# State-space mixer: the identity additions of two pairs of state columns issued together, behind every second pair

## Chip, cores and metric

The kernel runs on one core of one Trainium2 chip. The metric is the device time of one execution in microseconds; the comparison is between the kernel before and the kernel with the change below.

The engines are called by the names of the profile: PE is TensorE's matrix unit (PEld its weight loads), DVE is VectorE, ACT is ScalarE, POOL is GpSimd, SP is the engine that issues most transfers.

## What is computed

The whole program is a Perceiver-like stack of eleven layers over a (2, 256, 256) input and a (2, 4096, 256) context, all in float32. The change touches one layer, the state-space mixer. Cut to what matters, the reference of that layer is:

```python
delta = softplus(dtr @ W_dt + 2.0 * dt_bias).reshape(b, l, G, D_STATE)   # G = 32, D_STATE = 16
A = -exp(A_log).reshape(G, D_STATE, D_STATE)
a = exp(delta[..., None] * A)                       # decay of each state
bb = (delta * x)[..., None] * Bg[:, :, :, None, :]  # drive of each state
_, h = associative_scan(comb, (a, bb), axis=1)      # h[t] = a[t] * h[t-1] + bb[t]
y = einsum('blgpn,blgn->blgp', h, Cg)               # sum over the 16 state columns n
y = (y + D * xf) * silu(z)
return y @ W_out
```

There are 512 inner channels (four blocks of 128), 16 state columns per channel and 2 x 256 tokens. For each block and each state column the kernel makes a decay, a drive, a scan along the tokens, a product with C, and a sum over the 16 columns.

## The kernel before

The layer lies in one function, `l1_attn`. Channels lie on the 128 partitions, the 512 tokens (two sequences of 256) along the free dimension. The loop runs over 32 "pairs": a pair `k` is a block `j` of channels and two of its 16 state columns, so eight pairs make a block (k = 0 to 7 is block 0, and so on).

For a pair, five helper functions issue the work:

- `b_columns(k)` (L1332, L1340): two 32-row matmuls on PE spread the B values of the two columns over the partitions into two banks of the tag "tr" (two banks in all), and ACT copies each into a "spread" tile.
- `drives(k)` (L1349, L1351): ACT writes the decay exp(delta * A) of each column into a bank of the tag "dec" (two banks in all), POOL multiplies the spread tile by delta * x. Behind that it issues one step of the softplus of later blocks (`later`: an addition on ACT, L1224, and a product on POOL, L1225) as long as there are such steps.
- `states(k)` (L1332, L1365, L1369, L1370): two 32-row matmuls on PE spread the C values into two banks of the tag "mm" (three banks in all); DVE runs four scans (two columns, two sequences) into "state" tiles, and multiplies each column's state by its C bank. The order on DVE is scan, scan, scan, product of the first column (L1369), scan, product of the second column (L1370).
- `add_up(k)` (L1377): two matmuls with the identity on PE add the two weighed states into the bank `sums[j]` of the tag "acc" (one bank). Behind the eighth pair of a block DVE adds D * x (L1381) and POOL multiplies by silu(z) (L1384).
- `made` gives, in the first five iterations, one step each of the projections for blocks 1 to 3 (matmuls through L358, ACT copies L1292, L1295, L1296).

A float32 matmul stands as two passes in the trace, so a pair has four passes for its C columns, four for B columns and four for its additions.

Weighed states lie in tiles of the tag "state" in a pool of six buffers, so three pairs' worth; a tile comes free when the identity matmul that reads it has run. The loop is skewed: iteration `k` issues states of pair k, B columns of pair k + 2, decays and drives of pair k + 1, a step of `made`, and the additions of an earlier pair. The block stands under `in_order`, which ties each instruction of PE, DVE, ACT and POOL to the one issued before it on the same engine, so the order in the code is the order on each engine. The lines of the loop around the change:

```python
for k in range(-2, n + 1):          # n = 32
    if 0 <= k < n:
        states(k)
    if k + 2 < n:
        b_columns(k + 2)
    if 0 <= k + 1 < n:
        drives(k + 1)
    step = next(made, None)
    ...
```

After the loop `conv_hidden` issues the first matmuls of the next layer, and `linear` multiplies by W_out.

Of the kernel before, what the change touches and what calls it, by code (L numbers as in the profile page):

```python
# [268 lines left out]
class Perceiver:  # L269
# [960 lines left out]
    def l1_attn(self, x):  # L1230
# [5 lines left out]
        with ExitStack() as s:  # L1236
# [98 lines left out]
            def b_columns(k):  # L1335
                got = columns(mats["b"], bT, *pairs[k], "tr")
                spread[k] = []
                for ps in got:
                    spread[k].append(p4.tile([P, T], F32, name="spread", tag="spread"))
                    nc.scalar.copy(spread[k][-1], ps)  # L1340

            def drives(k):
                j, q, rs = pairs[k]
                decay[k], drive[k] = [], []
                for r, b in zip(rs, spread.pop(k)):

                    a = self.bank([P, T], "dec")
                    n = 16 * j + 4 * r + q
                    nc.scalar.activation(a, delta[:, j, :], AF.Exp, scale=neg_a[:, n : n + 1])  # L1349
                    decay[k].append(a)  # L1350
                    nc.gpsimd.tensor_mul(b, dx[:, j, :], b)  # L1351
                    drive[k].append(b)
                step = next(later, None)
                if step is not None:
                    step()

            def states(k):
                got = columns(mats["c"], cT, *pairs[k], "mm")
                weighed[k] = []

                for i, (a, bb) in enumerate(zip(decay.pop(k), drive.pop(k))):
                    h = p4.tile([P, T], F32, name="state", tag="state")
                    weighed[k].append(h)
                    for b in range(B):
                        nc.vector.tensor_tensor_scan(  # L1365
                            h[:, ts(b, L)], a[:, ts(b, L)], bb[:, ts(b, L)], 0.0, ALU.mult, ALU.add
                        )
                        if (i, b) == (1, 0):
                            nc.vector.tensor_mul(weighed[k][0], got[0], weighed[k][0])  # L1369
                nc.vector.tensor_mul(h, got[1], h)  # L1370

            def add_up(k):
                j, q, rs = pairs[k]
                if k % 8 == 0:
                    sums[j] = self.acc([P, T])
                for i, h in enumerate(weighed.pop(k)):
                    nc.tensor.matmul(  # L1377
                        sums[j], self.ident, h, start=k % 8 == 0 and i == 0, stop=k % 8 == 7 and i == 1
                    )
                if k % 8 == 7:  # L1380
                    nc.vector.scalar_tensor_tensor(  # L1381
                        yz[:, j, :], xr[:, j, :], self.col("ssm_d", j), sums[j], ALU.mult, ALU.add
                    )
                    nc.gpsimd.tensor_mul(yz[:, j, :], yz[:, j, :], zs[:, j, :])  # L1384

            e = mybir.EngineType
            with self.in_order(e.PE, e.DVE, e.Activation, e.Pool):
                n = len(pairs)
                for k in range(-2, n + 1):
# [6 lines that stand above are left out]
                    step = next(made, None)  # L1396
                    if step is not None:
                        step()
                    if k > 0:
                        add_up(k - 1)  # L1400
                self.conv_hidden("tr", "tr", "dec")
                return self.linear(yz, wout, x)
# [1196 lines left out]
```

## Time and profile before

| what | value |
|---|---|
| three runs, median | 2589.68 us |
| three runs, lowest and highest | 2589.52 and 2592.2 us |
| profiled execution, own time | 2594.41 us |
| profiled execution, span of its instructions | 2592.6 us |
| mean granted TensorE clock in it | 0.957 |
| busy over the span: PE, DVE, ACT, POOL | 95%, 66%, 52%, 36% |
| first scan and start of the last L1381 of the layer | 1320.4 and 1451.9 us |

Shares of the whole span average over eleven layers with different limits; the loop of the mixer lies between 1320 and 1452 us and is some 5% of the time. So it is read from views that are cut to that stretch. A start in the timeline is counted from the span's start. "issue" as the end of an idle time means that the profile shows nothing that was waited for. Matmuls are pipelined: one pass of 512 columns is listed as about 0.59 us while the next one starts sooner, so on PE starts are compared with starts.

### The profile page before, as it was taken

To read this page: it belongs to the slowest core of one execution; us is meant where nothing else is said; L and a number is where in the kernel's file an instruction comes from. 1 tells how busy PE (TensorE), PEld (TensorE's weight loads), DVE (VectorE), ACT (ScalarE), POOL (GpSimd) and SP (SyncE) were. 2 spreads that over 40 slices of the span, in tenths; PEclk is the share of its full clock that TensorE was granted. 3 is DMA by queue.
4 is the path that set the end of the run, shared out by engine and by line. 5 is a ranking of instruction groups with operands and counts; after the bars stand their busy time and mean duration, and the time that the engine had idled before them with its cause. 6 is when DMAs were issued, how large, how long until landed. Compare 5 with 4: busy or idle time off the path is not lost.

```text
span 2592.6 us, 51423 instructions
## 1 busy us (share of the span) xinstructions
PE 2457.8 (95%) x20579; PEld 1637.4 (63%) x20581; DVE 1709.5 (66%) x3184; ACT 1342.6 (52%) x2540; POOL 921.2 (36%) x864
## 2 busy tenths in 40 slices
PE   8987999999999999999799988899999999999889
PEld 6854566666666666666533556457935666664678
DVE  5566577777777777777579655444367888844542
ACT  3323666666666666666466322332116777783512
POOL 0520256656656656656459322001101222210010
PEclk9988999999999999999899998789999999998789
DMA  6210422222242222222300100006630000004556
GB/s 259 90 58 24 125 67 66 74 66 66 74 123 74 74 66 67 74 69 82 122 9 1 65 21 25 1 25 256 238 138 18 2 2 2 2 2 148 196 221 219
DMA packets 77278, 214.62 MB, mean 83 GB/s; under 512 B 6408, under 2 KB 21456, under 8 KB 66544
## 3 DMA queue, kind: packets, MB, share of 16 engines
q1 hardware_dynamic: 72128, 202.69, 23.4%
q0 software_dynamic: 1888, 5.90, 0.7%
q8 instruction: 162, 2.65, 0.4%
q10 hardware_dynamic: 3024, 2.75, 0.3%
q14 instruction: 76, 0.62, 0.1%
HBM read 190.48 MB, written 20.84 MB: 82 GB/s over the span
## 4 chain that ended last, share of the span: by engine, by line
PE 41%; DVE 5%; issue 2%; ACT 2%; POOL 1%; DMA 0%; DVEq 0%; ACTq 0%; POOLq 0%; SPq 0%
PE ps_mm L358 10%; PE ps_mm L2181 5%; PE ps_tr L2225 5%; PE ps_tr L2209 4%; PE ps_tr L358 3%; PE acc L358 3%; PE ps_mm L785 2%; PE ps_tr L2344 1%; DVE state L1365 1%; PE acc L826 1%; PE ps_tr L2387 1%; POOL spread L1351 1%; PE ps_tr L801 1%; PE acc L1377 1%; PE acc L1592 1%
## 5 line engine op out<-in xcount | busy, mean ns | idle before, releaser
L1092 POOL TENSOR_TENSOR total<-total,S 128x512 f32<-128x512 f32 x434 | 543.0, 1284 | 273.8 <-ACT S L1081 273.3
L1081 ACT ACTIVATE S<-S 128x512 f32<-128x512 f32 x512 | 302.6, 625 | 209.4 <-DVE S L1078 209.0
L2185 DVE TENSOR_REDUCE mx<-ps_mm 128x1 f32<-128x512 f32 x512 | 317.7, 683 | 71.5 <-PE ps_tr L2209 54.3
L1067 DVE TENSOR_TENSOR most<-ps_mm,most 128x512 f32<-128x512 f32 x448 | 278.1, 683 | 115.7 <-ACT S L1064 115.7
L1078 DVE TENSOR_TENSOR S<-S,ps_dec 128x512 f32<-128x512 f32 x512 | 317.2, 677 | 1.7 <-PE ps_dec L1136 1.7
L1064 ACT COPY S<-ps_mm 128x512 f32<-128x512 f32 x512 | 262.6, 599 | 99.8 <-PE ps_mm L1057 99.7
L2213 ACT ACTIVATE PT<-ps_tr 128x512 f32<-128x512 f32 x476 | 246.8, 602 | 74.6 <-PE ps_tr L2209 71.9
L1017 PEld LDWEIGHTS ps_tr<-w_l1x_wv,ctxT 128*64 128x64 f32 x4096 | 235.4, 137 | 58.4 <-issue 57.7
L1057 PE MATMUL ps_mm<-qT,kT 64*128 64x256 f32 x2048 | 255.7, 389 | 0.0
L1104 PE MATMUL acc<-S,v 128*64 128x256 f32 x2048 | 252.2, 385 | 0.7 <-DVE rec L1142 0.7
L2181 PE MATMUL ps_mm<-kT,qT 32*128 32x512 f32 x1024 | 249.7, 617 | 0.2 <-DVE mx L2185 0.2
L1017 PE MATMUL ps_tr<-w_l1x_wv,ctxT 128*64 128x128 f32 x4096 | 248.2, 273 | 0.0
L1017 PE MATMUL ps_tr<-ctxT,w_l1x_wk 128*64 128x512 f32 x1024 | 242.4, 593 | 0.4 <-PE ps_mm L1017 0.4
L2209 PE MATMUL ps_tr<-qm,kT 32*128 32x256 f32 x1904 | 238.2, 388 | 0.0
L1057 PEld LDWEIGHTS ps_mm<-qT,kT 64*128 64x128 f32 x2048 | 187.3, 186 | 44.1 <-issue 18.6
L1104 PEld LDWEIGHTS acc<-S,v 128*64 128x64 f32 x2048 | 139.1, 136 | 95.6 <-ACT S L1064 38.8
L2209 PEld LDWEIGHTS ps_tr<-qm,kT 32*128 32x128 f32 x1904 | 170.9, 184 | 16.2 <-issue 6.2
L2234 POOL TENSOR_TENSOR sums<-sums,part 128x256 f32<-128x256 f32 x102 | 73.8, 724 | 256.9 <-ACT part L2233 256.9
L2225 PE MATMUL ps_tr<-PT,v 128*32 128x256 f32 x2048 | 139.6, 385 | 0.3 <-ACT PT L2213 0.3
L1017 PEld LDWEIGHTS ps_tr<-ctxT,w_l1x_wk 128*64 128x64 f32 x1024 | 75.8, 137 | 91.3 <-issue 74.7
L335 DVE COPY v<-ps_tr 128x512 f32<-128x512 f32 x120 | 82.8, 690 | 71.4 <-PE ps_tr L1017 71.3
L2181 PEld LDWEIGHTS ps_mm<-kT,qT 32*128 32x128 f32 x1024 | 86.1, 184 | 60.0 <-issue 48.4
(543 smaller groups left out, 3817.9 us busy)
## 6 DMA issues: line engine op xcount, KB each, us to landing
ctxT<-in_ctxT SPq DMA_DIRECT2D x144, 512.0 KB, 3.6
ctxT<-in_ctxT SPq DMA_DIRECT2D x16, 1024.0 KB, 6.8
w_l2f_gu<-in_l2f_gu SPq DMA_DIRECT2D x16, 1024.0 KB, 7.4
bd_dram<-bd SPq DMA_DIRECT2D x8, 1536.0 KB
w_l3f_w<-in_l3f_w SPq DMA_DIRECT2D x11, 1028.0 KB, 8.4
w_l3f_w<-in_l3f_w SPq DMA_DIRECT2D x11, 1024.0 KB, 5.1
ctx<-in_ctx SPq DMA_DIRECT2D x8, 1024.0 KB, 6.1
w_l2f_down<-in_l2f_down SPq DMA_DIRECT2D x16, 512.0 KB, 4.3
```

What stands on the lines that cost most here:

```text
L358: self.nc.tensor.matmul(out, lhsT, rhs, start=i == 0, stop=i == len(pairs) - 1)
L1017: nc.tensor.matmul(ps[part], a[:, part], b, start=k == 0, stop=k == len(pairs) - 1)
L1057: nc.tensor.matmul(banks[hh, i][:, j, :], k[part, ts(2 * i + j, P)], q[u][part, :], start=True, stop=True)
L1067: nc.vector.tensor_tensor(m, ps, m, ALU.max)
L1078: nc.vector.tensor_tensor(t, t, spread[u][:, hh, :].unsqueeze(1).to_broadcast([P, 2, L]), ALU.add)
L1081: nc.scalar.activation(t, t, AF.Exp)
L1092: nc.gpsimd.tensor_add(tot, tot, t)
L1104: nc.tensor.matmul(av[u][part], vs[:, 2 * i + j, part], got[hh, i][:, j, :], start=g % 8 == 0 and i + j == 0, stop=g % 8 == 7 and i + j == 2,)
L2181: nc.tensor.matmul(ps, qT[rows, 2 * half + c, ts(t, P)], kT[rows, ts(j, 512)], start=True, stop=True,)
L2185: nc.vector.tensor_reduce(mx[:, c, r, j : j + 1], ps, AX.X, ALU.max)
L2209: nc.tensor.matmul(ps[:, i, :], kT[rows, ts(2 * u + i, P)], q[rows], start=True, stop=True)
L2225: nc.tensor.matmul(ps[ts(r, 32), :], v[:, 2 * u + i, :], pt[:, i, :], start=i == 0, stop=i == 1)
```

## The change

The additions of a pair were issued in the iteration after the pair. Now those of two pairs are issued together, in every second iteration: in iteration k = 2, 4, ..., 32 the additions of pairs k - 2 and k - 1. The additions of odd pairs keep their place; those of even pairs come one iteration later, directly ahead of those of the odd pair. Everything else, the order of the additions into `sums[j]` included, stays.

```diff
@@ -1396,7 +1396,9 @@
                     step = next(made, None)
                     if step is not None:
                         step()
-                    if k > 0:
+
+                    if k > 0 and k % 2 == 0:
+                        add_up(k - 2)
                         add_up(k - 1)
                 self.conv_hidden("tr", "tr", "dec")
                 return self.linear(yz, wout, x)
```

## Prediction

> **What bounds the kernel now.** I read four views, in this order. First the busy time by stretches, restricted to the state stage (start us:end us, length, then busy us and count of each engine, the granted clock, DMA share):
>
> ```profile
> 1342.00:1362.00 20.00, 20.00 (x64) 6.96 (x64) 18.76 (x32) 14.96 (x27) 17.80 (x15) 1.00 0.01 2
> 1362.00:1394.00 32.00, 32.00 (x104) 11.39 (x104) 30.91 (x51) 22.47 (x39) 31.90 (x27) 1.00 0.00 0
> 1394.00:1425.00 31.00, 31.00 (x100) 10.98 (x96) 29.97 (x50) 21.07 (x36) 29.77 (x25) 1.00 0.00 1
> ```
>
> PE never idles in the middle of the stage, DVE is 94 to 97% busy, POOL is full from 1362 to 1394. Three engines are level, so the order matters. Second, one iteration of the timeline (start, duration):
>
> ```profile
> 1346.47 1.85 DVE L1365 TENSOR_TENSOR_SCAN state<-ps_dec,spread 128x256 f32<-128x256 f32 x3
> 1346.52 1.13 PE L1332 MATMUL ps_mm<-cT,mat_c 32*128 32x512 f32 x4
> ...
> 1347.48 1.02 PE L1332 MATMUL ps_tr<-bT,mat_b 32*128 32x512 f32 x4
> ...
> 1348.24 0.66 DVE L1369 TENSOR_TENSOR state<-ps_mm,state 128x512 f32<-128x512 f32 x1
> 1348.43 1.98 PE L1377 MATMUL acc<-state,ident 128*128 128x512 f32 x4
> 1348.54 1.07 ACT L1340 COPY spread<-ps_tr 128x512 f32<-128x512 f32 x2 [1.01 <-PE ps_tr L1332]
> ...
> 1349.49 1.32 ACT L1349 ACTIVATE ps_dec<-delta,neg_a 128x512 f32<-128x512 f32 x2
> ```
>
> Write S(k) for the first scan of pair k, C(k), B(k) and A(k) for its c columns, b columns and additions. C(5) starts at 1346.52, B(7) 0.96 later, A(4) 0.95 after that, C(6) at 1350.35: PE's iteration is 0.96 + 0.96 + 1.91 = 3.83 us. The chain that releases the next pair is C(5) at 1346.52, B(7), its copies at 1348.54, the exponential at 1349.49, S(6) at 1350.30: C to next S is 3.78.
>
> Third, DVE later on: S is at 1362.61, 1393.63, 1424.48 and 1446.86 for k = 9, 17, 25, 31. From k = 26 to 31 that is 3.73 per pair, DVE's own floor (scans and products start about 0.59 apart, the last product waits 0.78 for the last scan). A pair with L1381 behind it takes 4.38. So S(31) is set by PE at first, by POOL around k = 9 to 17, by DVE at the end.
>
> Fourth, the waits in 1320 to 1343 and the start of the stage on PE:
>
> ```profile
> DVE state L1369 <- PE ps_mm L1332: 5.1, 3, 2.8
> ```
> ```profile
> 1326.17 1.13 PE L1332 MATMUL ps_mm<-cT,mat_c 32*128 32x512 f32 x4
> 1327.13 1.02 PE L1332 MATMUL ps_tr<-bT,mat_b 32*128 32x512 f32 x4
> 1328.82 1.13 PE L358 MATMUL ps_tr<-xc,mat_x 128*128 128x512 f32 x2 [0.67 <-ACT spread L1340]
> 1329.79 1.88 PE L1377 MATMUL acc<-state,ident 128*128 128x512 f32 x4
> 1331.60 1.13 PE L1332 MATMUL ps_mm<-cT,mat_c 32*128 32x512 f32 x4
> 1332.56 1.02 PE L1332 MATMUL ps_tr<-bT,mat_b 32*128 32x512 f32 x4
> 1333.51 3.70 PE L358 MATMUL ps_mm<-xT,win 128*128 128x512 f32 x8
> 1337.05 1.88 PE L1377 MATMUL acc<-state,ident 128*128 128x512 f32 x4
> 1338.86 1.13 PE L1332 MATMUL ps_mm<-cT,mat_c 32*128 32x512 f32 x4
> ```
>
> Here PE also carries the projections, and DVE waits 5.1 us for C. The third line matters beyond the start: a second user of the "tr" banks straight behind B(3) starts 1.69 after it, because the two banks are free only when ACT has copied them.
>
> [...]within a mode full-width matmuls start 0.43 apart, at each change about 0.1 is lost on either side, and the two 32-row halves of C start 0.01 apart. [...]a scan of 256 takes 0.676, a product of 512 takes 0.664. So DVE's floor stands whatever PE does.
>
> **The change, part by part.** *Counts.* No instruction is added or removed. Only A(k-2) for even k moves, from behind C(k-1), B(k+1) to behind C(k), B(k+2). It is four matmul passes; pairs with L1381 and L1384 have odd numbers, so those keep their place, and neither DVE's nor POOL's nor SP's queue is reordered. No DMA moves.
>
> *PE's own time.* Per two pairs the order is now C B (odd), C B A A (even). Two mode changes of 0.2 in place of four: 0.96 + 0.86 + 0.86 + 0.96 + 3.63 (1.91 and four more passes at 0.43) = 7.27, against 7.66. By itself it is a saving of 0.39 per two pairs.
>
> *What it meets.* B(o+2) of an odd pair o and B(o+3) now lie only one C apart. With C(o) at 0: B(o+2) starts 0.96, its copies start at 2.02 and 2.50 (1.06 and 0.48 as above), and the second is out, with a handover of 0.05, at 3.14. So the second half of B(o+3) starts at 3.14 rather than 2.68, ends its slots at 4.00, the mode change makes it 4.10, and eight passes of A take 3.63: **C(o+2) = C(o) + 7.73.** A second bound: the "mm" ring has three banks, so the second half of C(o+1) needs the product L1369 of pair o, which ends 2.43 after S(o); 0.05 of handover, two slots each of C and B (1.72), 0.1 and 3.63 give **C(o+2) = S(o) + 7.93.** Then S(o+1) = the later of S(o) + 3.73 and C(o) + 3.78. The two bounds are nearly equal, and both are above the 7.46 of DVE's floor: PE's saving is turned into waits, about 3.87 per pair.
>
> *L1381.* It waits for A(7), A(15), A(23), now at the end of eight passes. In the trace before it starts 0.11 after the C behind its A, and the next S comes 0.66 later: S(9) = C(9) + 0.77, likewise 17 and 25.
>
> *State buffers.* Six "state" tiles hold three pairs. S(o) overwrites the tile of A(o-3), which now runs up to an iteration later; in the steady part it is read some 2 us before it is needed. At the start S(3) waits for A(0) behind the projections (about 1337.1 against 1335.38), but C(3) decides there. Cost taken: nothing.
>
> *Start.* A(0) no longer stands before C(2): C(2) starts at 1329.88, B(4)'s second half at 1331.54 behind ACT's xr copy (1330.90 + 0.58), the projections at 1332.5, A(0) and A(1) at 1336.04, C(3) 3.53 later at 1339.57 against 1338.86. S(4) = 1343.35, S(5) = 1347.08 against 1346.47: **0.61 lost.** C(5) = 1347.30.
>
> *Sum.* From C(5) and S(5) the rules give, by steps of two:
> S(7) 1354.81, S(9) 1363.53, S(17) 1395.42, S(25) 1427.31, S(31) 1450.48. Before: 1362.61, 1393.63, 1424.48, 1446.86 for the last four. The loss grows 0.92, 1.79, 2.83, **3.62 us.** POOL's slips at k = 10 and 18 (0.34 and 0.28 above 3.73) are under the new waits and are not counted again. The tail is unchanged: after C(31) come A(30), A(31) in both orders, and the last A waits for DVE's last product either way.
>
> The profiled execution took 2594.41 (span 2592.6, 1.8 around it); with 3.6 added 2598.0. The median of the runs shown, 2589.68, is 4.7 below it. I give **2593.3** on the scale of the median, +0.14%. A measurement of this kernel can tell 0.2% (5.2 us) from no change; less counts as the same.
>
> **Bounds of the unknown.** Not shown before: B behind B with one C between, with both halves under waits. If the halves overlap so that nothing is lost, PE's 7.27 is under DVE's floor. S(31) cannot come before 27 pairs at 3.73 and three L1381 at 0.65 after S(4) = 1342.64, that is 1445.3: 1.5 gained, and with the start and the later L1381 kept, about 1 lost. If the halves exclude each other, another 0.5 is lost in each of 13 rounds.
>
> **Rivals.**
> *A: waits eat the saving, as summed.* For: the 0.67 wait behind B(3), and the late second half of C(31), whose last pass ends 1.45 after its first starts, not 1.13. +3.6, 2593.3, from -0.5 to +5.1. Chance 0.74.
> *B: the loop locks, slower.* Place: the second half of B(o+3) behind ACT's second copy and of C(o+1) behind L1369. [...]if the waiting half also stops its partner, a round costs 7.73 + 0.5 = 8.2; 13 rounds add 6.6 to 3.6: +10, 2599.9. It decides once a round is above about 7.85. For: DVE waits in the same loop (S behind the exponential). Against: C(31) shows that a half lags alone. Chance 0.22.
> *C: the mode changes were the bound, faster.* 16 times 0.39 is 6.2 us of PE, 2583.5. Against: DVE's floor leaves 1.5, so 2588.2 is the most I see, which still counts as the same. Over 5.2 faster needs a wrong floor: 0.04.
> That the change is not carried out is excluded: the loop stands in an order imposed on PE, DVE, ACT and POOL.
>
> **Numbers.** Faster 0.04, same 0.74, slower 0.22. The range runs from just inside the floor, 2589.0, to 2598.5, which takes in half of the way to B's end.
>
> **What would show it.** A in runs of eight passes; C to C alternating near 2 and 5.8; PE for the first time idle in mid-stage, behind ACT's copies and L1369; S about 3.87 apart; L1381 waiting for A three times in mid-stage; S(31) some 130 after S(0) (before 126.45). Wrong if PE stays without gaps, if S runs at 3.73 from k = 5, or if a round is over 8.

## The result, and the profile after

The changed kernel takes 2605.74 us, median of six runs (2602.77 to 2613.11), against 2590.32 for the kernel before beside it; the ratio is 1.0061 (1.0049 to 1.0073; here and below the brackets behind a ratio hold its 95% interval). A second set gave 2605.03 against 2591.72, ratio 1.0051 (1.0036 to 1.0065). The forecast was +0.14%, 2593.3 us, with a range up to 2598.5; the kernel is 0.5 to 0.6% slower, beyond that range.

The stage is measured from S(0) to S(31), the first scans of the first and the last pair. It took 126.45 us before (126.44 in a second profile) and 138.34 and 141.66 us in two profiles of the change: 11.9 and 15.2 us more, which is roughly the 15.4 and 13.3 us between the medians. S(0) itself came at 1320.4 before and at 1325.3 in the first profile after, although nothing ahead of it changed; over the ten later profiles it lay between 1320.0 and 1323.0. So only the stage is compared below.

First the same view as before: busy time by stretches of the changed kernel (first profile). The columns are start and end, length, then busy us and count of PE, PEld, DVE, ACT and POOL, the granted clock, DMA share and GB/s.

```profile
1342.00:1362.00 20.00, 19.80 (x65) 7.56 (x63) 16.93 (x28) 11.24 (x20) 13.84 (x12) 1.00 0.00 0
1362.00:1394.00 32.00, 30.34 (x84) 11.55 (x83) 26.79 (x44) 19.42 (x35) 27.37 (x23) 0.89 0.00 1
1394.00:1425.00 31.00, 29.51 (x90) 11.33 (x89) 27.83 (x46) 19.61 (x36) 29.96 (x26) 0.94 0.00 1
1425.00:1447.00 22.00, 20.54 (x64) 7.87 (x64) 20.29 (x34) 12.92 (x23) 18.05 (x15) 1.00 0.00 0
1447.00:1470.00 23.00, 22.30 (x60) 7.94 (x54) 18.20 (x30) 9.77 (x16) 8.20 (x8) 0.93 0.00 1
```

Two things are new. PE has gaps (30.34 of 32 us where it had 32.00), which the forecast said. And the granted clock, 1.00 in every stretch before, is 0.89, 0.94 and 0.93 in three of them. The record of the clock behind that column has three drops to one half inside the stage: 6.8 us from 1372.3, 3.4 us from 1416.7 and 3.4 us from 1450.8. The second profile has four, 20.5 us in all. Before there is none.

One round of the change, from its timeline (start, duration):

```profile
1352.37 1.15 PE L1332 MATMUL ps_mm<-cT,mat_c 32*128 32x512 f32 x6
...
1353.33 1.02 PE L1332 MATMUL ps_tr<-bT,mat_b 32*128 32x512 f32 x4
...
1354.38 1.07 ACT L1340 COPY spread<-ps_tr 128x512 f32<-128x512 f32 x2 [1.69 <-PE ps_tr L1332]
...
1354.55 0.69 PE L1332 MATMUL ps_mm<-cT,mat_c 32*128 32x512 f32 x1 [0.20 <-DVE state L1369]
...
1355.02 0.69 PE L1332 MATMUL ps_tr<-bT,mat_b 32*128 32x512 f32 x1
...
1355.51 1.12 PE L1332 MATMUL ps_tr<-bT,mat_b 32*128 32x512 f32 x3
...
1356.56 3.70 PE L1377 MATMUL acc<-state,ident 128*128 128x512 f32 x8
```

C(5) starts at 1352.37, B(7) 0.96 later. The second half of C(6) starts at 1354.55, when L1369 of pair 5 has freed its bank, 2.18 behind C(5); B(8) starts at 1355.02 and 1355.51, each half as ACT's copy frees a bank; the eight additions come at 1356.56. C(7) follows at 1360.19: a round of 7.82 us. The wait that ends last is the one for ACT's second copy. The round before shows it, in which S(3) is further ahead of C(3) and L1369 frees its bank sooner:

```profile
1344.54 1.15 PE L1332 MATMUL ps_mm<-cT,mat_c 32*128 32x512 f32 x6
1346.45 1.12 PE L1332 MATMUL ps_mm<-cT,mat_c 32*128 32x512 f32 x2
...
1348.73 3.70 PE L1377 MATMUL acc<-state,ident 128*128 128x512 f32 x8
```

Here the second half of C(4) starts 1.91 behind C(3) instead of 2.18, and the additions still start 4.19 behind it, as in the other round. The list of waits (window 1325 to 1470; total us, times, longest) names L1369 as what PE idles for; while the second half of B waits for ACT, PE has passes of C and of the other half of B to run, so that wait leaves no idle time on PE (0.18 and 0.20 us on PEld in the round from C(5)):

```profile
PEld ps_mm L1332 <- DVE state L1369: 16.0, 14, 2.1
...
DVE state L1365 <- ACT ps_dec L1349: 15.4, 13, 10.2
...
PE ps_mm L1332 <- DVE state L1369: 4.8, 8, 1.3
...
DVE state L1365 <- PE acc L1377: 3.8, 2, 3.5
...
DVE low L1381 <- PE acc L1377: 2.2, 4, 1.2
```

And this is a drop of the clock in the same kernel: the 3.40 us ahead of it, and the drop; then two runs of eight additions from the timeline, one ahead of the drop and one under it.

```profile
1368.90:1372.30 3.40, 2.13 (x12) 0.74 (x8) 3.30 (x6) 2.06 (x4) 3.40 (x3) 1.00 0.00 0
1372.30:1379.10 6.80, 6.80 (x10) 2.33 (x8) 5.89 (x10) 2.68 (x5) 6.80 (x7) 0.50 0.00 0
```
```profile
1364.38 3.70 PE L1377 MATMUL acc<-state,ident 128*128 128x512 f32 x8
...
1373.95 6.28 PE L1377 MATMUL acc<-state,ident 128*128 128x512 f32 x8
```

Eight passes that take 3.70 us take 6.28, the last of them behind the drop; at the other two drops they take 5.40. C(11) then starts 3.82 us behind S(11), where a normal round has 0.30, and S(12) comes 7.66 us after S(11).

### The profile page after: what moved, and what is told of

The parts are those of the page before. It is cut to its first block, busy times and chain, and to the rows that moved or that the text cites. A ratio compares the mean times of both kernels' runs of the same rounds, so it can differ in the third digit from the quotient of the medians.

```text
span 2604.2 us, 51423 instructions
## 1 busy us (share of the span) xinstructions
PE 2464.6 (95%) x20579; PEld 1641.3 (63%) x20581; DVE 1710.0 (66%) x3184; ACT 1341.3 (52%) x2540; POOL 920.6 (35%) x864
## 4 chain that ended last, share of the span: by engine, by line
PE 43%; DVE 5%; ACT 2%; issue 1%; DMA 0%; DVEq 0%; ACTq 0%; SPq 0%
PE ps_mm L358 10%; PE ps_mm L2183 5%; PE ps_tr L2227 5%; PE ps_tr L2211 4%; PE ps_tr L358 3%; PE acc L358 3%; PE acc L1377 2%; PE ps_mm L785 2%; PE ps_tr L2346 1%; PE ps_tr L1332 1%; PE ps_mm L1332 1%; PE acc L826 1%; DVE state L1365 1%; PE ps_tr L2389 1%; PE ps_tr L801 1%
```

## Experiments

**The same two kernels again.** No edit.

> The changed kernel once more, for a second profile. The stage is read from the first scan of pair 0, S(0), to that of pair 31, S(31): 126.45 us before, 138.35 in the first profile of the change. Theory 1 (waits plus clock): PE now idles in the loop behind the product L1369 and ACT's copies, which costs 4 to 5 us by itself, [...] So the stage takes 133 to 140 us, with 2 to 4 drops of the clock in it, not all at the same pairs. Theory 2 (buffers): the six state tiles hold DVE up; then DVE's waits for L1377 are the largest in the stage. Theory 3 (elsewhere): the loss lies outside the stage, as the 4.9 us by which S(0) is later in the first profile; then it differs from profile to profile and the stage does not hold the difference of the medians.

> The kernel before once more, for a second profile and for the spread of unchanged code. Theory 1: stage 126 to 127.5 us with no drop of the clock between 1320 and 1450, ratio to itself 1.000 within 0.001; the time of S(0) may move by some us, since it hangs on drops of the clock in the layers ahead. Theory 3: stage times spread by more than 5 us between profiles.

Measured: the change's stage 141.66 us with four drops (6.8 us from 1367.0, 3.4 from 1387.4, 6.8 from 1404.5, 3.4 from 1448.9); the kernel before 126.44 us and no drop, ratio of its runs to the others 0.9997 (0.9987 to 1.0008). The 141.66 is above the 140 expected; the fourth drop makes it. Every gap between scans outside the drops is the same in both profiles of the change within 0.02 us. So the stage of before repeats to 0.01 us, that of the change repeats except for drops of the clock, and DVE's waits for L1377 (4.2 us in three waits here, 3.8 in two in the first profile) are not the largest. The loss is in the stage. Theories 2 and 3 do not fit this.

**Filler in the gaps.** The change, with two 32-row matmuls of zeros into the block's sum, ahead of the even pair's c columns; not in the first round of a block, where the sum's bank is not yet open.

```diff
+            def fill(k):
+                j = pairs[k - 2][0]
+                rows = ts(3, 32)
+                for _ in range(2):
+                    nc.tensor.matmul(sums[j], zero[rows, :], cT[rows, j, :], start=False, stop=False)
...
+                    if 0 < k < n and k % 2 == 0 and k % 8 != 2:
+                        fill(k)
                     if 0 <= k < n:
                         states(k)
```

> The change, with two 32-row matmuls of a zero matrix on the fourth row group, added into the block's sum (they add zero), between the b columns of the odd pair and the c columns of the even pair: where PE idles. 12 of the 16 rounds have them. Theory 1: PE works on in its gaps and the clock stays at 1.0 in most of the stage; S(0) to S(31) falls from about 138 to 131 to 133 us (the waits remain), the time by 5 to 8 us against the change. Theory 2 and theory 3: no gain; each filler of 0.86 us on PE can only add, up to 12 times 1.7 us if other row groups do not run beside it.

Measured: stage 136.64 us, 2600.19 us, ratio 1.0035 (1.0021 to 1.0049). Better than the change, not as good as expected: two drops are left, 6.8 us from 1367.6 and 3.4 us from 1405.1, both in the first round of a block, where the filler was left out. The other rounds keep the full clock. More work on PE made the stage shorter, by 1.7 and 5.0 us against the two profiles of the change.

**Late, but not grouped.** The kernel before, with the additions of every pair one iteration later, one pair at a time.

```diff
-                for k in range(-2, n + 1):
+                for k in range(-2, n + 2):
...
-                    if k > 0:
-                        add_up(k - 1)
+                    if k > 1:
+                        add_up(k - 2)
```

> The kernel before, with the additions of every pair one iteration later, but one pair per iteration (C, B, A as before, with A of the pair two back). Additions are as late as in the change, the state tiles as tight, and there is no run of eight. Theory 1: PE's order of work is that of before, 3.83 us per pair, no new wait for L1369, no drop of the clock: stage 126 to 127.5 us, and the end one or two us later, since the last two runs of additions and the last L1381 come together only behind the last pair; ratio to before 1.000 to 1.001. Theory 2: the scans wait for L1377, and a good part of the 12 us is there without any grouping.

Measured: stage 125.46 us, no drop, 2589.44 us, ratio 0.9989 (0.9980 to 0.9998). The stage is shorter than the 126 to 127.5 us expected. Lateness with six state tiles costs nothing and gains a little: one run of additions fewer stands ahead of C(3), which starts 17.52 us behind S(0) where it was 18.45 before, and S(5) comes at 25.12 us, not 26.06. What costs is the grouping.

**What stood ahead of the drops.** In the clock's records of the kernel before and of the change, every drop inside the span but the last lasts 3.41, 6.83, 10.24, 13.65 or 20.48 us. So for each profile I laid a grid of 3.41 us on those records over the stage, and summed in each cell the matmul passes (0.43 us each at full clock), weighted by their rows: 1 for the additions (128 rows), 0.25 for c and b columns and filler (32 rows). The sum, as a part of the cell, is called its share below; it is an estimate of mine from the starts in the traces, and the weights are my choice. Cells ahead of a drop, in both profiles of the change and in the filled kernel: 0.27 to 0.40. Cells that stayed at full clock in those: 0.39 or more; in the kernel before 0.58 or more, except one cell at 0.43 among the projections at the start (1326.1). Grouping makes cells in which no addition starts, or hardly any (none in the cell ahead of the first drop of the change, one pass in each of those ahead of the other two). Two simpler measures do not sort the cells. One is the time in which some matmul ran: a cell of the change with 0.88 of it (1447.4) was followed by a drop, one with 0.63 (1437.2) was not. The other is whether an addition falls in the cell: two cells of the change without one (1396.2 and 1430.4, shares 0.40 and 0.39) kept the clock.

**Filler everywhere.** The filled kernel, with filler also in the first round of a block, where it opens the bank. The lines are against the filled kernel.

```diff
-                    if 0 < k < n and k % 2 == 0 and k % 8 != 2:
+                    if 0 < k < n and k % 2 == 0:
                         fill(k)
```

> The filler of the run before, now in all 16 rounds: in the first round of a block it opens the sum's bank, so that the windows behind L1381, which were still bare, are filled too. Theory 1 in its sharper form: [...] Weighted by the rows of the array that are in use, the windows ahead of the seven drops of the two profiles of the change stand at 0.27 to 0.40, those without a drop at 0.39 or more, those of the kernel before at 0.58 or more inside the loop. With every gap filled (about 0.5): no drop, stage 130.5 to 132.5 us (126.45 plus the waits of 5 us), ratio to before 1.001 to 1.003. Rival: the clock follows time without any matmul, which the filler hardly changes behind L1381 (PE waits 1.27 us there in any case): drops remain at pairs 9 to 11 and 17 to 19, stage 136 or more.

Measured: no drop, stage 131.61 us, 2594.87 us, ratio 1.0014 (1.0007 to 1.0021), all as the sharper theory expected. It does not yet decide against the rival, whose premise failed: behind the first L1381, from 1363.7 to 1367.1, PE is busy for 3.40 us of 3.40, where the change had 2.13 of 3.40 in the stretch shown above. So the filler raised the time with a matmul as well as the share. Its busy time by stretches:

```profile
1362.00:1394.00 32.00, 32.00 (x113) 14.03 (x112) 29.85 (x50) 21.19 (x37) 30.77 (x26) 1.00 0.00 1
1394.00:1425.00 31.00, 31.00 (x110) 13.60 (x109) 28.86 (x48) 20.25 (x36) 30.33 (x25) 1.00 0.00 0
1425.00:1447.00 22.00, 22.00 (x76) 9.52 (x76) 20.58 (x34) 11.36 (x21) 15.01 (x13) 1.00 0.00 1
```

The clock is 1.00 everywhere, and DVE is at 93% where it was at 97% before: the rounds of 7.82 are still there, and C(17) to C(19) takes 8.80 us where the change takes 8.79 at full clock, so the filler itself costs nothing. This separates the two costs: 131.61 - 126.45 = 5.2 us for the waits, the rest for the clock. One sum fits every profile of the change and its filled forms: 131.5 us (fitted) and half of the time at half clock. 131.5 + 13.7/2 = 138.3 (measured 138.34), + 20.5/2 = 141.7 (141.66), + 10.2/2 = 136.6 (136.64).

**Grouping without a run of eight.** The change, with A(k-2) ahead of B(k+2) and A(k-1) behind it.

```diff
                         states(k)
+                    if k > 0 and k % 2 == 0:
+                        add_up(k - 2)
                     if k + 2 < n:
                         b_columns(k + 2)
...
-                        add_up(k - 2)
                         add_up(k - 1)
```

> The change with A(k-2) put ahead of B(k+2) and A(k-1) behind it: order C B C A B A. Additions are as late and as tight in buffers as in the change, no run of eight, four changes of mode per two pairs as before, B never close behind B. What stays is C of the even pair directly behind C, B of the odd pair, so its second half waits for L1369. Waits theory: that wait alone makes a round of 2.43 + 0.96 + 1.91 + 0.96 + 1.91 = 8.17 us against 7.66 of before, worse than the 7.82 of the change without drops: stage 131.5 to 134 us, no or one drop of the clock. If the wait for ACT's copies, B behind B, is what costs in the change, or the run of eight: a round of 7.66 to 7.7, stage 126 to 127.5.

Measured: stage 142.30 us with two drops (10.2 us), so about 137.2 without, 2604.44 us, ratio 1.0047 (1.0032 to 1.0062). The direction is as expected and the size is not: a round is 8.42, not 8.17, and there were two drops where none or one was expected. A round from PE's timeline:

```profile
1385.36 1.15 PE L1332 MATMUL ps_mm<-cT,mat_c 32*128 32x512 f32 x6
1386.32 1.02 PE L1332 MATMUL ps_tr<-bT,mat_b 32*128 32x512 f32 x4
1387.84 1.12 PE L1332 MATMUL ps_mm<-cT,mat_c 32*128 32x512 f32 x2 [0.50 <-DVE state L1369]
1388.89 1.98 PE L1377 MATMUL acc<-state,ident 128*128 128x512 f32 x4
1390.81 1.13 PE L1332 MATMUL ps_tr<-bT,mat_b 32*128 32x512 f32 x4
1391.87 1.98 PE L1377 MATMUL acc<-state,ident 128*128 128x512 f32 x4
1393.78 1.15 PE L1332 MATMUL ps_mm<-cT,mat_c 32*128 32x512 f32 x6
```

Here B never follows B, and the wait for L1369 (0.50 us of PE in this round) ends last. The 0.25 us over the expected 8.17 are in these lines: 2.48 us from C to the late half (1385.36 to 1387.84) where the sum had 2.43, 1.05 us for the late half (1387.84 to 1388.89) where the sum had 0.96, and 1.06 for B between two runs of additions (1390.81 to 1391.87) where it had 0.96. So in this order the wait for L1369 is enough to make the loop longer than the change does. It does not show that this wait sets the rounds of the change: there ACT's second copy comes last, except in the first round of a block.

**More state tiles.** The change with eight of them.

```diff
-                    h = p4.tile([P, T], F32, name="state", tag="state")
+                    h = p4.tile([P, T], F32, name="state", tag="state", bufs=8)
```

> The change with eight state tiles in place of six. Waits theory: S(3) comes earlier by 1 to 2 us, since it no longer waits for A(0), but S(4) and S(5) stay at 23.0 and 26.76 us behind S(0), because C(3) sets them; a round stays at 7.82, and drops of the clock stay: stage 135 to 142. Buffer theory: the rounds shrink towards 7.5 and the stage to 128 or less.

Measured: stage 138.35 us, with drops of 13.7 us in all, as in the first profile of the change. S(3) comes at 13.56 us behind S(0) rather than 16.87, more than the 1 to 2 us expected, S(5) at 26.76 in both. The 3.5 us wait for a state tile is hidden behind C(3).

**Time without a matmul, or share of the array?** Two kernels in the order of before. Both leave out the additions of the six middle pairs of each block and repeat c-column matmuls in their place, on one row group or on two.

```diff
                 got = columns(mats["c"], cT, *pairs[k], "mm")
+                j, q, rs = pairs[k]
+                for i, ps in ((0, got[0]),) * 2:        # two groups: ((0, got[0]), (1, got[1])) * 2
+                    rows = ts(rs[i], 32)
+                    nc.tensor.matmul(ps, mats["c"][rows, ts(q, P)], cT[rows, j, :], start=True, stop=True)
...
+                    if 0 < k % 8 < 7:
+                        continue
```

> What lets the clock fall: too little of the array in use, or too much time without a matmul? The order of before; the additions of the six middle pairs of each block are left out, and to keep PE occupied in time the first of the two c-column matmuls of each pair is issued three times over (the same values into the same bank). At DVE's pace of 3.73 us a pair PE has 32-row work for 0.86 (C) + 1.72 (the repeats, on one row group) + 0.86 (B) = 3.44 us, 0.92 of the time, more than the 0.84 to 0.89 of windows that dropped in the change; weighted by rows it is (0.43 + 0.43 + 0.43) / 3.73 = 0.35. Share of the array: drops in the middle of every block, clock at one half for a third or more of the stage. Time without a matmul: no drop.

> The same, with the additions of the middle pairs left out, but both c-column matmuls issued three times over, on two row groups side by side. The time that PE is occupied stays at 0.92, the share weighted by rows rises to (0.43 + 0.86 + 0.43) / 3.73 = 0.46. Share of the array: above the 0.40 up to which windows dropped, so the clock stays at 1.0. Time without a matmul: the same as with one group. Both kernels: DVE sets the pace while the clock is full, stage 118 to 124 us, since the start carries less on PE.

Measured: with one group the clock is at one half for 157 us in three stretches from 1349.7 on, past the end of the stage, which takes 185.05 us; with two groups for 51 us of a stage of 162.10 us. The second expectation failed: PE waits for banks there (5.7 us in six waits for DVE's first product), and in four cells the share stood at 0.35 to 0.38 and the clock fell. Neither stage is the 118 to 124 us expected at DVE's pace. The clearest case is one cell of the kernel with one group, by stretch, and the additions that follow it:

```profile
1373.50:1377.00 3.50, 3.50 (x13) 1.38 (x10) 2.95 (x6) 0.05 (x1) 3.15 (x3) 0.99 0.00 0
```
```profile
1376.84 3.68 PE L1383 MATMUL acc<-state,ident 128*128 128x512 f32 x4
```

PE ran matmuls through the whole stretch (0.97 of the cell by pass starts), with a share of 0.38, and the clock was at one half from 1377.0: four passes take 3.68 us where they take 1.98. So here the clock fell with hardly any time without a matmul ahead of it. In both kernels every drop in the stage follows a cell at 0.26 to 0.38, and no cell under 0.39 kept the clock. In the kernel above with A apart one cell at 0.37 kept it and one at 0.41 did not: by my weights, the shares ahead of a drop and those of cells that kept the clock overlap.

**A version with a shorter stage.** The kernel before, with each pair's additions two iterations later, one pair at a time, and with eight state tiles.

```diff
-                    h = p4.tile([P, T], F32, name="state", tag="state")
+                    h = p4.tile([P, T], F32, name="state", tag="state", bufs=8)
...
-                for k in range(-2, n + 1):
+                for k in range(-2, n + 3):
...
-                    if k > 0:
-                        add_up(k - 1)
+                    if k > 2:
+                        add_up(k - 3)
```

> The kernel before with each pair's additions two iterations later (A of the pair three back, one pair per iteration), and eight state tiles. The kernel with one iteration more took 0.9989 of before, its stage 125.46 against 126.45: PE's projections at the start come first, and L1381 is no longer waited for. Waits theory: another 1.9 us of additions leaves the start, S(5) comes 23 to 24.5 us behind S(0) (26.06 before, 25.12 with one iteration), later POOL and DVE take most of it back: stage 123.5 to 125.5, ratio to before 0.998 to 1.000. If lateness costs anything, it is slower than the kernel with one iteration.

Measured: stage 123.75 us, S(5) at 23.40, 2588.32 us, ratio 0.9989 (0.9981 to 0.9997). All within what was expected; it is 2.7 us shorter in the stage than before and, within what the medians tell, no faster than one iteration later. Both are about 0.1% under the kernel before, less than the 0.2% that the forecast called a change.

## Why the prediction was wrong

**The missing term.** The step that failed is the price of PE's passes. The sum took every pass of PE at the 0.43 us of the trace before, where the clock stood at 1.0 through the stage. That the clock could fall to one half once the additions are gathered was in no step and in no rival, nor in the range. The lower clock is worth 138.34 - 131.5 = 6.8 us and 141.66 - 131.5 = 10.2 us in two profiles. Filling the gaps took it away whole: with the clock full and the grouping kept, the kernel stands at 1.0014. That this is the forecast's own +0.14% is in part luck, since the stage lost 5.2 us there and not the 3.62 of the sum; the interval, 0.07 to 0.21%, holds both. The drops in the stage of the change last 3.4 or 6.8 us. The clock fell behind cells in which matmuls ran for 0.51 to 0.97 of the time, but nearly all of them on a quarter of the rows each. The prediction did not ask what C, B, C, B without an addition, 4.19 us from C to the next addition in a round, would be to the clock. In the kernel before, where the clock stands at 1.00, each 3.83 us hold one run of four additions, 1.91 us from its start to the next C.

**PE's own time.** Right in structure: runs of eight at 3.63 to the next C, two changes between 32-row and full-width passes in place of four, and the saving turned into waits.

**The two bounds of a round.** The rule from C, 7.73, sets an ordinary round, and it was mis-sized by 0.09. The second half of B(8) starts 3.14 behind C(5) (1355.51 and 1352.37), as summed; from there to the additions it takes 1.05 us (1355.51 to 1356.56), where the sum had 0.96. I let the late half cost two slots of 0.43; its second pass starts 0.53 after its first. So a round is 7.82. The rule from S sets only the first round of a block, where L1381 holds S back behind C, and was as much too small: C(19) comes 8.02 behind S(17) (1412.47 and 1404.45), not 7.93. With 7.82 and 8.02 and the measured start, the prediction's own recursion gives a stage of about 131.3 us by my estimate; the kernel with the clock full has 131.61. So the waits are worth 5.2 us where the sum had 3.62. By itself this would have left the time inside the range.

**L1381.** Right: S(9) came 0.77 behind C(9), and L1381 waited for A four times, three in mid-stage and once at the end. **State tiles.** Right: S(3) is held 3.5 us, and eight tiles change nothing from S(4) on. **Start.** S(5) 26.76 us behind S(0) against 26.06: 0.70 lost, forecast 0.61. **Tail.** Right: last A and L1381 as before.

**The rivals.** A was the mechanism of 5.2 of the 12 to 15 us. B, a round of 8.2 in which a waiting half stops its partner, did not happen: ordinary rounds at full clock take 7.82 to 7.88 us. The change is slower even than B's 2599.9, but through the clock. (The 8.42 with A apart come from another order of work.) C did not happen: even with the clock full and the grouping kept the kernel takes 1.0014 of before.

**What stays open.** What sets the clock is not shown: the share is my estimate, with weights of mine, and its ranges were found on the same few profiles that they describe. The spread of the time outside the stage (some 5 us) lies beside drops of the clock in other layers and was not studied; ahead of S(0) the clock stood at one half for 61.4 us in the profile before and for 71.7 us in the first one after.

## What to carry to other kernels

An order of work on PE can set more than its waits. In this case, gathering full-array work into runs of eight saved changes between 32-row and full-width passes (0.2 us each: in the kernel before, starts lie 0.52 and 0.53 us apart ahead of and behind the first addition of the run at 1348.43, and 0.43 within the run) and cost half of the clock for 3.4 or 6.8 us at a time. So where full-array and narrow matmuls alternate, lay the record of the granted clock beside the order of work. Before a run of narrow matmuls is put directly behind another, see which bank each half waits for, and which of these waits ends last. A list of waits shows only those in which the engine idles: here L1369 leads what PE and PEld wait for from other engines (16.0 us), though ACT's second copy ended last.

## What was not expected of the hardware

In the kernel with one group the granted clock fell to one half behind a stretch through which PE ran matmuls (3.50 us of 3.50 from 1373.5 to 1377.0), the share of that cell being 0.38 by my weights. Filler of zeros on one row group, four passes or 1.7 us of it in each round, ran beside other row groups (with filler everywhere, a pass of it and one of C both start at 1357.04), and the clock stood at 1.00 from 1342 to 1447: a stage of 131.61 us in place of 138.34 or 141.66.

Matmuls on different row groups did not start in the order of the code: in the change the first half of C(6) stands behind C(5) and B(7) in the code; in the timeline six passes of C start at 1352.37 to 1352.93, two more than C(5) has, ahead of B(7) at 1353.33. The section on the kernel before takes the order in the code for the order on each engine, and the prediction's sum does so too. The six passes disagree, as far as the trace can tell: it does not name the pair of a pass, and the two are told from their count. With filler ahead of C(6), that half no longer runs ahead (four passes at first, in both filled kernels); why is open. It did not change the sum, since the second half of C(6) waits in any case.
